# A two-layer graph attention network: the scatter matmuls of a step ahead of the next step's spreading, with index work behind the one-hots

## The chip, the cores and the metric

The kernel runs on one core of one Trainium2 chip. The metric is the time of one execution in microseconds (us); the kernel before takes 4928.91 us (median of three runs, 4916.35 to 4935.57). A core has five engines with an instruction queue each, worked through in order: TensorE (PE in the profile, its weight loads PEld), VectorE (DVE), ScalarE (ACT), GpSimd (POOL) and SyncE (SP). Engines wait for each other by semaphores.

## The reference

A graph attention network of two layers on 6250 nodes with 256 features and 200000 edges, sorted by destination node. Cut to what matters (`src`, `dst` are the edge list, `ea` 32 features per edge; layer 0 has four heads, layer 1 one):

```python
h = maximum(layernorm(x), 0)
for l in (0, 1):
    te  = relu(ea @ We[l] + be[l]) * exp(h @ Wo[l] + bo[l])[src][:, None]
    # one self loop per node, its te the mean of the node's incoming te
    hx  = (h @ Wg[l]).reshape(n, heads, f)
    al  = leaky_relu((hx . a_s)[src] + (hx . a_d)[dst] + (te @ Wge[l]) . a_e, 0.2)
    al  = exp(al - segment_max(al, dst)[dst])
    al /= segment_sum(al, dst)[dst]
    out = segment_sum(hx[src] * al, dst) + b[l]
    h   = relu(out + h) if l == 0 else out + h
return x + (h + maximum(layernorm(x), 0))
```

## The kernel before

**Tiling.** The edges of a layer are cut into chunks of 128 (an edge to a partition), and 24 chunks make a step; 66 steps make a layer (the last two are shorter). Since edges are sorted by destination, the edges of one step belong to a run of at most some hundred nodes, and a node that is cut by a step's border is carried to the next step as one row (`carried`).

**One step** consists of these parts (names of the code; lines of the profile):

- `gather` (L1065): 24 indirect DMAs on POOL fetch the source rows of the edges into `G`, one of three buffers in turn. The gathers of step j+3 use the buffer of step j and wait for its last scatter matmul.
- `spread` (L1189, L1190): one-hots `lb` and `Q` on DVE that spread a node's destination term to its edges, made for two steps at a time; `parts` (L1296 to L1304): that term in three bf16 parts, and a matmul with `Q`; `blocks` (L1311): its result multiplied into `aq`.
- `rphase1` (L1165, L1166): edge features through the edge matrix, `y` on PE and relu into `R` on ACT, in two pieces (256 columns, then 512, called y1 and y2 below). `rphase2` (L1174): `R` through a second matrix into the PSUM bank `zad`. `adst` (L1318): `aq` and `lb` added into the same bank.
- `edge_rows` and `logits` (L1332 to L1363, DVE): `zad` transposed, added to the gathered source terms, leaky relu, and running maxima; `ends` (L1370, PE) transposes chunk ends into the PSUM tile `lf`; `links` (L1380, L1382 DVE, L1387 PE) joins maxima over chunks; `maxima` (L1397 to L1423, DVE, with the exp on ACT) gives each edge its weight.
- `scale` (layer 0: one DVE instruction over all 24 chunks, L1454) or `scale_rows` (layer 1: 24 ACT instructions, L1463) multiplies `G` by the weights; `carried` (L1436 to L1444, DVE) adds the carried row.
- `onehots` (L1283, DVE): `S`, which edge belongs to which node; `sums` (L1473, PE): 24 matmuls of `S` with `G` into `u`, two records each in the profile; `evict` (L1478, ACT) copies `u` out.
- `finish` (DVE, L1489 to L1640 in layer 0, L1494 to L1585 in layer 1): the nodes of a step that is done; in layer 0 `rows1` (L1563 on PE), `rows2` (L567) and `rows3` (L571 on DVE) turn them into the rows that layer 1 gathers. `index_on` (L748 to L779, DVE): up to seven instructions that make the index tables of the next group of four steps, in layer 0 only.

**Order.** The function `edges` writes the instructions of a whole run in program order, and each engine executes its own in that order. The loop is software-pipelined: iteration k finishes step `st` = k (logits onwards) and prepares step `nx` = k+1 (spread, parts, rphase1, rphase2, adst, onehots, edge_rows). In one iteration of the kernel before the order is: gather(nx), logits(st), ends(st), spread(nx), parts(nx), y1(nx), links(st), rows2, blocks(nx), maxima(st), y2(nx), rphase2(nx), adst(nx), scale(st), carried(st), sums(st), rows3, onehots(nx), finish(step k-1), evict(st), rows1(k-1), index_on, edge_rows(nx). The first and the last three steps of a layer have their own sequences.

## Time and profile before

| what | before |
|---|---|
| time, median of three runs | 4928.91 us (4916.35 to 4935.57) |
| the profiled execution | 4925.46 us, span 4923.7 us |
| PE, DVE, POOL, ACT busy | 60%, 50%, 61%, 23% of the span |
| weight loads (PEld), beside the matmuls | 37% |
| mean granted TensorE clock | 0.725 of full speed |
| DMA packets | 248253, 591.97 MB |

No engine is busy all the time, and the busy shares don't say which one sets the pace. In rows of a timeline the first number is the start, the second the busy time of the group, then engine, line, operation, output and inputs, partitions by elements, the count, and in brackets the engine's idle time ahead of the row with what ended it; "issue" there means that the engine waited for nothing that the profile shows.

### The profile page before, as it was taken

Reading aid. Unit: us, or ns where it says so; the run is one execution under the profiler, and the core shown is the slowest. Engines: PE = TensorE matmul, PEld = TensorE weight load, DVE = VectorE, ACT = ScalarE, POOL = GpSimd, SP = SyncE. Lnnn points to the kernel's source line nnn. Section 1 sums busy time; section 2 is a strip of 40 time slices with the busy share of each in tenths; the row PEclk is TensorE's granted clock in tenths of the full one; section 3 lists DMA queues with packets and bytes.
Section 4 is the critical chain, followed back from the end, with each engine's and each line's share of the span. In section 5 each row is a group of like instructions: output and inputs, shape, how many; then the busy total and the mean of one; then the engine's idle time right before and its main releaser. Section 6 shows DMA issues by size and latency. Waiting matters only on the chain.

```text
span 4923.7 us, 38114 instructions
## 1 busy us (share of the span) xinstructions
PE 2940.4 (60%) x10100; PEld 1841.8 (37%) x10100; DVE 2462.7 (50%) x6148; ACT 1132.2 (23%) x2701; POOL 2989.0 (61%) x3216
## 2 busy tenths in 40 slices
PE   6655666666666666665646556555565555655656
PEld 5433433343333434343434333333333333333334
DVE  5556666676666666666734323333333332333335
ACT  4211111111111111111103323233233332323322
POOL 6356666666666666666544656656666666666663
PEclk8777777777777777777777667667667676666767
DMA  7144444444444444444433434434444443443442
GB/s 223 55 119 125 126 128 134 123 135 132 133 124 128 135 126 131 129 135 122 122 109 92 121 106 115 122 105 119 114 118 114 112 121 107 116 118 107 118 117 71
DMA packets 248253, 591.97 MB, mean 120 GB/s; under 512 B 65849, under 2 KB 105125, under 8 KB 247783
## 3 DMA queue, kind: packets, MB, share of 16 engines
q0 software_dynamic: 150048, 422.51, 32.7%
q1 hardware_dynamic: 97009, 164.82, 10.5%
q10 hardware_dynamic: 976, 2.12, 0.2%
q8 instruction: 86, 1.41, 0.1%
q14 instruction: 134, 1.10, 0.1%
HBM read 544.23 MB, written 45.36 MB: 120 GB/s over the span
## 4 chain that ended last, share of the span: by engine, by line
issue 29%; PE 28%; DVE 21%; POOL 13%; another core or an unknown queue 5%; DMA 3%; ACT 1%; SPq 0%; DVEq 0%; ACTq 0%; POOLq 0%
PE u L1473 21%; POOL G L1065 12%; DVE G L1454 7%; DMA G<-T,src 3%; PE y L1165 2%; DVE S L1283 2%; PE zad L1174 2%; DVE m L1402 1%; DVE lb L1189 1%; DVE rt L1332 1%; ACT R L1166 1%; DVE t1rows L1638 1%; DVE fb L1397 0%; PE lf L1370 0%
## 5 line engine op out<-in xcount | busy, mean ns | idle before, releaser
L1065 POOL DMA_INDIRECT G<-T,src x3066 | 2912.9, 950 | 1824.8 <-issue 949.2
L1473 PE MATMUL u<-G,S 128*128 128x270 f32 (+1 forms) x6212 | 1873.3, 448 | 1419.9 <-issue 1202.2
L1473 PEld LDWEIGHTS u<-G,S 128*128 128x128 f32 x6212 | 1355.8, 221 | 1871.8 <-issue 1438.5
L1463 ACT ACTIVATE G<-G,kw 128x256 f32<-128x256 f32 x1512 | 609.0, 496 | 0.0
L1380 DVE TENSOR_TENSOR_SCAN cl<-fl,cl,lf 4x129 f32<-4x129 f32 (+1 forms) x130 | 61.1, 470 | 1007.6 <-PE zad L1304 940.1
L1478 ACT ACTIVATE U<-u 128x270 f32<-128x270 f32 (+1 forms) x130 | 51.0, 393 | 2169.3 <-PE u L1473 1686.5
L1454 DVE TENSOR_TENSOR G<-G,kps 128x6144 f32<-128x6144 f32 (+6 forms) x86 | 441.7, 5150 | 0.0
L1283 DVE TENSOR_TENSOR S<-kps,loc 128x3072 f32<-128x3072 f32 (+1 forms) x135 | 438.1, 3245 | 4.7
L1165 PE MATMUL y<-ea,webd 64*128 64x256 f32 (+2 forms) x1056 | 355.0, 762 | 41.0 <-ACT R L1166 35.3
L1174 PE MATMUL zad<-R,wea 128*64 128x384 f32 (+1 forms) x1056 | 285.0, 677 | 156.6 <-issue 87.5
L1166 ACT ACTIVATE R<-y,webd 128x1024 f32<-128x1024 f32 (+3 forms) x264 | 235.4, 892 | 427.5 <-PE y L1165 161.9
L1174 PEld LDWEIGHTS zad<-R,wea 128*64 128x64 f32 x1056 | 82.9, 177 | 395.8 <-issue 263.4
L1505 DVE SCALAR_TENSOR_TENSOR mg<-U,mw 128x1 f32<-128x1 f32 x65 | 14.4, 221 | 364.1 <-remote 170.6
L1165 PEld LDWEIGHTS y<-ea,webd 64*128 64x128 f32 x1056 | 116.0, 269 | 105.6 <-issue 59.3
L1332 DVE STREAM_TRANSPOSE rt<-zad 128x768 f32<-128x768 f32 (+1 forms) x130 | 125.8, 968 | 5.4 <-remote 5.4
L567 PE MATMUL fin<-wg,h1T 128*128 128x260 f32 x264 | 116.8, 587 | 1.5 <-ACT h1T L1565 1.5
L1189 DVE TENSOR_TENSOR lb<-lb,kps 128x1536 bf16<-128x1536 bf16 (+1 forms) x68 | 112.9, 1661 | 0.0
L1436 DVE SCALAR_TENSOR_TENSOR G<-U,kw,G 1x257 f32<-1x257 f32 x62 | 29.5, 476 | 152.4 <-issue 87.0
L1575 ACT ACTIVATE t1rows<-t1rows 128x1 f32<-128x1 f32 x66 | 13.4, 203 | 363.9 <-DVE t1rows L571 147.4
L1370 PE MATMUL lf<-ident,fb 128*36 128x128 f32 (+1 forms) x132 | 52.0, 394 | 55.8 <-DVE fb L1363 45.6
L1318 PE MATMUL zad<-lb,aq 128*128 128x384 bf16 (+2 forms) x264 | 83.8, 409 | 0.0
L1515 ACT ACTIVATE mw<-mw 128x8 f32<-128x8 f32 x66 | 13.8, 209 | 298.7 <-issue 146.9
(275 smaller groups left out, 2366.7 us busy)
## 6 DMA issues: line engine op xcount, KB each, us to landing
ea<-in_ea_dram SPq DMA_DIRECT2D x64, 768.0 KB
G<-T,src POOLq DMA_INDIRECT x3066
lb<-locrow SPq DMA_DIRECT2D x64, 384.0 KB
nd<-t1rows SPq DMA_DIRECT2D x66, 225.8 KB
tw<-nd SPq DMA_DIRECT2D x66, 225.8 KB
tw<-T SPq DMA_DIRECT2D x66, 117.2 KB
T<-t1rows SPq DMA_DIRECT2D x66, 113.8 KB
tw<-in_x_dram SPq DMA_DIRECT2D x66, 112.0 KB
```

The costliest lines, as they stand in the source:

```text
L567: self.nc.tensor.matmul(ps[:, :L.MW], hT[:, k, :], self.wg[L.l][:, k, :], start=(k == 0), stop=(k == 1))
L1065: nc.gpsimd.indirect_dma_start(out=G[:, c, 0:L.TW], out_offset=None, in_=st.get("from", self.T[L.l])[0:self.N, :], in_offset=bass.Indirect ...
L1165: nc.tensor.matmul(y[:, i, :n], self.webd[l][r, :], ea[r, w], start=True, stop=True)
L1166: nc.scalar.activation(R[:, :, w], y[:, :, :n], AF.Relu, bias=self.be[l])
L1174: nc.tensor.matmul(st["zad"][i * PH:(i + 1) * PH, o], self.wea[l][0], R[:, i, w], start=True, stop=False)
L1189: V.tensor_tensor(lb[:, :, :n], lb[:, :, :n], self.k_part.unsqueeze(2).to_broadcast([P, i, n]), op=OP.is_equal)
L1283: nc.vector.tensor_tensor(st["S"][:, c0:c1, :], self.k_iota.unsqueeze(1).to_broadcast(w), self.loc[:, o + c0:o + c1].unsqueeze(2).to_broad ...
L1318: self.nc.tensor.matmul(st["zad"][:, o], st["aq"].rearrange("p k j -> p (k j)"), st["lb"][:, w], start=False, stop=True)
L1332: V.transpose(rv[:, :32 * c].rearrange("p (b n) -> p b n", b=2), z.rearrange("p (b n) -> p b n", b=2)[:, :, :16 * c])
L1454: nc.vector.tensor_tensor(v, v, pw[:, c0:c1, :].unsqueeze(3) .to_broadcast([P, c1 - c0, H, L.F]), op=OP.mult)
L1463: self.nc.scalar.activation(v, v, AF.Copy, scale=st["w"][:, c:c + 1])
L1473: nc.tensor.matmul(st["u"][:, :L.W], S[:, i, :], G[:, i, 0:L.W], start=(j == 0), stop=(j == c - 1))
```

## The change

In iterations k from 1 on, `links`, `maxima`, the scaling and `carried` of the step come ahead of `spread`, `parts`, `blocks` and `adst` of the next. `parts` then writes its matmul into free columns of the bank of `lf` instead of `zad`. Layer 0 and layer 1 now have different sequences:

- Layer 0: y2 and rphase2(nx) right behind maxima; the scaling in two instructions of 12 chunks with `carried` between them; then spread(nx), 14 chunks of sums, parts(nx), blocks(nx), 5 chunks of sums, adst(nx), the last 5 chunks.
- Layer 1: scale_rows ahead of the second piece of `R`; 8 chunks of sums, with spread and parts of the next step behind them, the other 16 chunks; then rphase2(nx), onehots(nx), blocks(nx) and adst(nx), so that edge_rows(nx) and the next logits, which read `zad`, come behind all of the sums.
- In both, index_on stands right behind the one-hots, ahead of finish, evict and rows1. k = 0 keeps its order.

```diff
--- before.py
+++ after.py
@@ -821,8 +821,9 @@
                 st["rows"] = st["L"].l
                 drain(self.logits(st))
                 self.ends(st)
-            self.spread(nx)
-            self.parts(nx)
+            else:
+                self.spread(nx)
+                self.parts(nx)
             y = self.rphase1(nx)
             next(y)
             if k:
@@ -830,33 +831,59 @@
             if late:
                 self.rows2(late)
             self.load_fl(k + 1)
-            self.blocks(nx)
             if k:
                 drain(self.maxima(st))
-            drain(y)
-            self.load_ea(k + 2)
-            self.rphase2(nx)
-            self.adst(nx)
+            else:
+                self.blocks(nx)
+            if k and st["rows"]:
+                self.scale_rows(st)
+                drain(y)
+                self.load_ea(k + 2)
+            else:
+                drain(y)
+                self.load_ea(k + 2)
+                self.rphase2(nx)
             if "S" not in st:
                 self.onehots(st)
-            if k:
-                if st["rows"]:
-                    self.scale_rows(st)
-                else:
-                    drain(self.scale(st))
+            if not k:
+                self.adst(nx)
+                self.onehots(nx)
+            elif st["rows"]:
                 self.carried(st)
-                self.sums(st)
+                self.sums(st, (0, C // 3))
+                self.spread(nx)
+                self.parts(nx, self.lf)
+                self.sums(st, (C // 3, C))
+                self.rphase2(nx)
+                self.onehots(nx)
+                self.blocks(nx)
+                self.adst(nx)
+            else:
+                f = self.scale(st, cuts=(0, C // 2, C))
+                next(f)
+                self.carried(st)
+                drain(f)
+                self.spread(nx)
+                self.sums(st, (0, 14))
+                self.parts(nx, self.lf)
+                self.blocks(nx)
+                self.sums(st, (14, 19))
+                self.adst(nx)
+                self.sums(st, (19, C))
+                if late:
+                    self.rows3(late)
+                    late = None
+                self.onehots(nx)
             if late:
                 self.rows3(late)
                 late = None
-            self.onehots(nx)
+            self.index_on(left)
             if pv:
                 drain(self.finish(pv))
             self.evict(st)
             if pv:
                 self.rows1(pv)
                 late = pv
-            self.index_on(left)
             if k == 4 and self.early:
                 self.lacking()
             if k >= 6:
@@ -1166,8 +1193,14 @@
             nc.scalar.activation(R[:, :, w], y[:, :, :n], AF.Relu, bias=self.be[l])
             yield
 
+    def zad(self, st):
+
+        if "zad" not in st:
+            st["zad"] = self.ps_1.tile([P, 1024], F32, name="zad")
+
     def rphase2(self, st):
 
+        self.zad(st)
         nc, l, R = self.nc, st["L"].l, st["R"]
         for w, o in self.halves(st):
             for i in range(2):
@@ -1283,7 +1316,7 @@
             nc.vector.tensor_tensor(st["S"][:, c0:c1, :], self.k_iota.unsqueeze(1).to_broadcast(w),
                                     self.loc[:, o + c0:o + c1].unsqueeze(2).to_broadcast(w), op=OP.is_equal)
 
-    def parts(self, st):
+    def parts(self, st, bank=None):
 
         L, V = st["L"], self.nc.vector
         H = L.H
@@ -1300,8 +1333,10 @@
             for j, t in enumerate(q):
                 t["a3"] = a3[:, j]
         a3 = st["a3"]
-        st["zad"] = z = self.ps_1.tile([P, 1024], F32, name="zad")
-        self.nc.tensor.matmul(z[:, 400:400 + 3 * H], st["Q"], a3[:, :H, :].rearrange("p h t -> p (h t)"),
+        if bank is None:
+            self.zad(st)
+        st["ad"] = z = st["zad"][:, 400:400 + 3 * H] if bank is None else bank[:, 240:240 + 3 * H]
+        self.nc.tensor.matmul(z, st["Q"], a3[:, :H, :].rearrange("p h t -> p (h t)"),
                               start=True, stop=True)
 
     def blocks(self, st):
@@ -1309,7 +1344,7 @@
         H = st["L"].H
         st["aq"] = aq = self.aq[st["k"] % 2]
         self.nc.vector.tensor_tensor(aq[:, :, 4:4 + 3 * H],
-                                     st["zad"][:, 400:400 + 3 * H].unsqueeze(1).to_broadcast([P, 4, 3 * H]),
+                                     st["ad"].unsqueeze(1).to_broadcast([P, 4, 3 * H]),
                                      self.quad.unsqueeze(2).to_broadcast([P, 4, 3 * H]), op=OP.mult)
 
     def adst(self, st):
```

In layer 0, PE's queue reads so before, from a step's end to its sums (u is the scatter's sum, y and R the edge features, zad the edge terms, fin the node rows):

```order
L1563 MATMUL fin<-ident,fb 128x128 x2
L1370 MATMUL lf<-ident,fb_195 36x128
L1304 LDWEIGHTS Q
L1304 MATMUL zad<-a_6577,Q 128x12
L1165 MATMUL y<-ea,webd_119 128x256 x2
L1387 MATMUL lf<-ident,cl_189 128x36
L567 MATMUL fin<-wg_894,h1T 128x260 x2
L1165 MATMUL y<-ea,webd_119 128x512 x2
L1174 MATMUL zad<-R,wea_142 64x384 x4
L1318 LDWEIGHTS aq_199
L1318 MATMUL zad<-lb,aq_199 128x384
```

and so after, from y2 on (L1192 is the old L1165, L1207 the old L1174, L1508 the sums, L1339 parts, L1353 adst):

```order
L1192 MATMUL y<-ea,webd_119 128x512 x2
L1207 MATMUL zad<-R,wea_142 64x384 x4
L1508 MATMUL u<-G,S 128x270 x14
L1339 LDWEIGHTS Q
L1339 MATMUL lf<-a_7320,Q 128x12
L1508 MATMUL u<-G,S 128x270 x5
L1353 LDWEIGHTS aq_198
L1353 MATMUL zad<-lb,aq_198 128x384
L1353 LDWEIGHTS aq_198
L1353 MATMUL zad<-lb,aq_198 128x384
L1508 MATMUL u<-G,S 128x270 x5
```

The parts matmul and the adst matmuls have moved from ahead of the sums into them; DVE's `blocks`, which needs the former, therefore waits for 14 chunks of sums.

DVE's queue in layer 0, in a step without spreading, from the scaling on, before:

```order
L1454 TENSOR_TENSOR G<-G,kps 128x24x256
L1439 TENSOR_TENSOR crow<-U,kps 1x256
L1442 TENSOR_TENSOR crow<-U,kps 1x4
L1443 TENSOR_TENSOR G<-G,crow 1x260
L1444 SCALAR_TENSOR_TENSOR G<-U,slink,G 1x5
L571 TENSOR_TENSOR t1rows<-fin,bias_898 128x260
L1280 COPY kps<-lastloc 128x1
L1283 TENSOR_TENSOR S<-kps,loc 128x3072
L1489 TENSOR_SCALAR cnt<-U 128x1
```

and after (L1489 is now the scaling, L1346 blocks, L1316 the one-hots, L748 the first instruction of index work):

```order
L1489 TENSOR_TENSOR G<-G,kps 128x12x256
L1474 TENSOR_TENSOR crow<-U,kps 1x256
L1477 TENSOR_TENSOR crow<-U,kps 1x4
L1478 TENSOR_TENSOR G<-G,crow 1x260
L1479 SCALAR_TENSOR_TENSOR G<-U,slink,G 1x5
L1489 TENSOR_TENSOR G<-G,kps 128x12x256
L1346 TENSOR_TENSOR aq_199<-lf,quad 128x4x12
L571 TENSOR_TENSOR t1rows<-fin,bias_898 128x260
L1313 COPY kps<-lastloc 128x1
L1316 TENSOR_TENSOR S<-kps,loc 128x3072
L748 CAST gf<-gi 128x192
```

The row of `blocks` now stands ahead of everything that DVE does for node rows, one-hots and the next logits; before, it stood ahead of maxima.

PE's queue in layer 1, one step, before:

```order
L1370 MATMUL lf<-ident,fb_195 33x128
L1304 LDWEIGHTS Q
L1304 MATMUL zad<-a_12796,Q 128x3
L1165 MATMUL y<-ea,webd_900 128x256 x2
L1387 MATMUL lf<-ident,cl_189 128x33
L1165 MATMUL y<-ea,webd_900 128x512 x2
L1174 MATMUL zad<-R,wea_145 64x384 x4
L1318 LDWEIGHTS aq_199
L1318 MATMUL zad<-lb,aq_199 128x384
L1318 LDWEIGHTS aq_199
L1318 MATMUL zad<-lb,aq_199 128x384
L1473 MATMUL u<-G,S 128x261 x24
```

and after:

```order
L1508 MATMUL u<-G,S 128x261 x8
L1339 LDWEIGHTS Q
L1339 MATMUL lf<-a_21417,Q 128x3
L1508 MATMUL u<-G,S 128x261 x16
L1207 MATMUL zad<-R,wea_145 64x384 x4
L1353 LDWEIGHTS aq_199
L1353 MATMUL zad<-lb,aq_199 128x384
L1353 LDWEIGHTS aq_199
L1353 MATMUL zad<-lb,aq_199 128x384
L1405 MATMUL lf<-ident,fb_195 33x128
L1192 MATMUL y<-ea,webd_900 128x256 x2
```

The matmuls into zad of the next step (its own rows aside, the same number) stand behind the sums, directly ahead of the transpose L1405 (before: L1370) that needs the logits made from them.

## The prediction

> **What bounds the kernel now.** First the page, its chain and its costliest groups.
>
> ```profile
> issue 29%; PE 28%; DVE 21%; POOL 13%; another core or an unknown queue 5%; DMA 3%; ACT 1%; SPq 0%; DVEq 0%; ACTq 0%; POOLq 0%
> L1473 PE MATMUL u<-G,S 128*128 128x270 f32 (+1 forms) x6212 | 1873.3, 448 | 1419.9 <-issue 1202.2
> ```
>
> No engine owns the chain. The sums carry most of PE's idle time, and it is put down to "issue": PE waits for nothing that the profile shows. So I looked at the beat of the steps, in the timeline of POOL: the first gather of a step, first and last regular step of layer 0, then of layer 1.
>
> ```profile
> 335.12 0.94 POOL L1065 DMA_INDIRECT G<-T,src  x1 [24.97 <-PE fin L1563]
> ...
> 1229.18 0.94 POOL L1065 DMA_INDIRECT G<-T,src  x1 [4.61 <-PE fin L1563]
> ...
> 1258.39 0.95 POOL L1065 DMA_INDIRECT G<-T,src  x1 [0.30 <-issue]
> 1267.51 0.94 POOL L1065 DMA_INDIRECT G<-T,src  x1 [8.18 <-PE u L1473]
> ...
> 1301.98 0.94 POOL L1065 DMA_INDIRECT G<-T,src  x1 [4.62 <-PE fin L1563]
> ...
> 2374.07 0.99 POOL L1065 DMA_INDIRECT G<-T,src  x1 [5.59 <-PE u L1473]
> ...
> 2699.18 0.94 POOL L1065 DMA_INDIRECT G<-T,src  x1 [8.29 <-PE zad L1304]
> ...
> 4801.97 0.94 POOL L1065 DMA_INDIRECT G<-T,src  x1 [7.21 <-PE zad L1304]
> ```
>
> Layer 0: 2038.95 us in 57 steps, 35.77 each. Layer 1: 2102.79 us in 58 steps, 36.25 each. A step's 24 gathers run back to back at 1.25 us, about 30 us (1229.2 to 1259.3 here); then POOL waits until the sums of the step that holds its next buffer end. I call the time from burst start to burst start T, and the time from burst start to the first sums matmul S. A faster S only pays if it ends the sums earlier, so next the sums in PE's timeline, layer 0, a late step and an ordinary one:
>
> ```profile
> 1244.87 9.93 PE L1473 MATMUL u<-G,S 128*128 128x270 f32 x36 [3.30 <-DVE G L1444]
> ...
> 1263.03 4.21 PE L1473 MATMUL u<-G,S 128*128 128x270 f32 x9 [1.49 <-issue]
> ...
> 1279.01 11.99 PE L1473 MATMUL u<-G,S 128*128 128x270 f32 x45 [4.59 <-DVE crow L1442]
> ...
> 1297.20 0.61 PE L1473 MATMUL u<-G,S 128*128 128x270 f32 x1 [2.41 <-issue]
> ...
> 1301.59 0.42 PE L1370 MATMUL lf<-ident,fb 128*36 128x128 f32 x1
> ```
>
> This is the central observation. 45 of 48 records run in 12 us; then they come 2.8 us apart, until some 3.5 us after the last gather, and after that what is left runs fast again (9 records in 4.2 us). I call it the slow stretch; the trace shows it on all queues, not its cause. Two bounds on a step follow. The late step (S = 1244.87-1229.2 = 15.7) still has 9 records when the stretch ends, and T is 38.3. The ordinary one (S = 11.5) is done at 1297.8, half a microsecond after the burst, and gains nothing by it: PE gets on at 1301.6 and POOL at 1302.0, T = 34.5. In the steps of layer 0 T never falls under 34.4; I take 34.45 as a floor. Of 57 steps 15 have T over 37 (mean 38.39), the other 42 a mean of 34.84.
>
> For the cause of a late S, DVE's timeline:
>
> ```profile
> 1230.55 0.33 DVE L1363 TENSOR_TENSOR_SCAN fb<-pen,al 128x96 f32<-128x96 bf16 x1
> ...
> 1233.48 0.47 DVE L1380 TENSOR_TENSOR_SCAN cl<-fl,cl,lf 4x129 f32<-4x129 f32 x1
> ...
> 1267.92 0.47 DVE L1380 TENSOR_TENSOR_SCAN cl<-fl,cl,lf 4x129 f32<-4x129 f32 x1 [1.41 <-PE zad L1304]
> ...
> 1271.43 6.54 DVE L1454 TENSOR_TENSOR G<-G,kps 128x6144 f32<-128x6144 f32 x1
> ...
> 1278.74 0.20 DVE L1444 SCALAR_TENSOR_TENSOR G<-U,slink,G 1x5 f32<-1x5 f32 x1
> ...
> 1289.93 0.98 DVE L1332 STREAM_TRANSPOSE rt<-zad 128x768 f32<-128x768 f32 x1
> ...
> 1299.61 0.33 DVE L1363 TENSOR_TENSOR_SCAN fb<-pen,al 128x96 f32<-128x96 bf16 x1
> ```
>
> In the late step DVE ends the logits at 1230.9, 1.7 after the burst began, and spreads for 2.7 ahead of links. In the ordinary one it was done in time, and the chain is links, maxima, scaling, carried: 1267.9 to 1278.9. DVE has little to spare: from 1289.93 the last eight instructions of the logits take 10 us, in the slow stretch.
>
> **The change in layer 0.** Half of the scaling goes behind carried: 6.54/2 = 3.27 off the path. blocks (short, 0.2 as L1444) and, in every second step, spread and the parts casts (2.7) leave the path to links. So S falls from 11.5 to about 8.0, if the logits are in time. Two costs stand against it.
>
> DVE's cover: blocks now waits for the parts matmul behind 28 records, 28 x 12/45 = 7.5 us from S, so at +15.8 in a step; the one-hots and the node rows, which began at 1278.9 (+11.4), begin at about +16, 4.6 later, and the second half of the scaling and the spreading (6.0) lie in that gap. Everything behind them, logits last, moves to the right, into the slow stretch. Before, the logits ended at +32.4 (1299.9); now I expect some +35, and with seven instructions of index work +37 or +38 (before, such a step had them 1.7 past the next burst's start: the late step above). Against T = 34.5 they are 0.5 to 3.5 late, which gives S = 8.5 to 11.5, not 8.0.
>
> PE: parts (two instructions) and adst lie in the sums; the number of instructions ahead of the last sums matmul is the same, so I count nothing, bounds 0 and +1 a step.
>
> S of 8.5 to 11.5 is where T stood at 34.4 to 35. I take 34.75 for all 57: 57 x (35.77-34.75) = -58. Bounds: all at the floor, 57 x 1.32 = -75; or DVE so late that S is 12 to 13 everywhere, where T was about 36 in the few steps of before that started so: 57 x 0.23 = +13.
>
> index_on goes ahead of finish (7 x 0.3, with L1363 for a short instruction, is 2 us) and no longer stands between finish and edge_rows: the same queue, the same sum, 0 for the logits, but rows1 on PE comes 2 later; PE waits for the logits there anyway. rows3 keeps its place behind the sums, and so do its stores on SP. Of load_ea and load_fl on SP only the place in layer 1 changes, behind the scaling; they fetch a later step's data, 0. One scaling more costs one instruction's start, covered by DVE's wait for blocks. No row of POOL's queue moves.
>
> **The change in layer 1.** Here zad and adst leave the front of the sums and come behind them. Burst starts of a step with fast and one with slow matmuls ahead of its sums, then PE in the latter, all engines in the former, and its logits:
>
> ```profile
> 3644.12 0.94 POOL L1065 DMA_INDIRECT G<-T,src  x1 [7.25 <-PE zad L1304]
> ...
> 3679.13 0.94 POOL L1065 DMA_INDIRECT G<-T,src  x1 [5.21 <-PE zad L1304]
> ...
> 4112.78 0.94 POOL L1065 DMA_INDIRECT G<-T,src  x1 [7.28 <-PE zad L1304]
> ...
> 4149.45 0.94 POOL L1065 DMA_INDIRECT G<-T,src  x1 [6.90 <-PE zad L1304]
> ```
>
> ```profile
> 4118.01 2.83 PE L1174 MATMUL zad<-R,wea 128*64 128x384 f32 x8 [1.22 <-issue]
> ...
> 4120.78 0.82 PE L1318 MATMUL zad<-lb,aq 128*128 128x384 bf16 x2
> ...
> 4121.39 8.56 PE L1473 MATMUL u<-G,S 128*128 128x261 f32 x37
> ...
> 4145.94 3.25 PE L1473 MATMUL u<-G,S 128*128 128x261 f32 x6 [2.23 <-issue]
> ...
> 4149.30 0.70 PE L1165 MATMUL y<-ea,webd 64*128 64x256 f32 x4
> ```
>
> ```profile
> 3644.09 0.47 DVE L1380 TENSOR_TENSOR_SCAN cl<-fl,cl,lf 1x129 f32<-1x129 f32 x1 [12.33 <-PE zad L1304]
> ...
> 3646.26 0.23 ACT L1419 ACTIVATE kw<-mt 128x25 f32<-128x25 f32 x1 [0.77 <-DVE mt L1410]
> ...
> 3647.73 9.66 ACT L1463 ACTIVATE G<-G,kw 128x256 f32<-128x256 f32 x24
> 3647.89 1.51 PE L1174 MATMUL zad<-R,wea 128*64 128x384 f32 x8 [1.22 <-ACT R L1166]
> ...
> 3648.66 0.20 DVE L1444 SCALAR_TENSOR_TENSOR G<-U,slink,G 1x2 f32<-1x2 f32 x1
> ...
> 3649.33 0.50 PE L1318 MATMUL zad<-lb,aq 128*128 128x384 bf16 x2
> 3649.66 8.53 PE L1473 MATMUL u<-G,S 128*128 128x261 f32 x38
> ```
>
> ```profile
> 3659.26 0.97 DVE L1332 STREAM_TRANSPOSE rt<-zad 128x768 f32<-128x768 f32 x1
> ...
> 3661.69 0.18 DVE L1363 TENSOR_TENSOR_SCAN fb<-pen,al 128x24 f32<-128x24 bf16 x1
> ```
>
> Before, S is 5.5 (3649.66-3644.12) with T = 35.0, or 8.6 (4121.39-4112.78) with T = 36.7; of the 58 steps 11 are of the first kind, 36 of the second, and 11 lie between at S = 7.3 with T about 35.6. The mean S is 7.8.
>
> New chain from the last sums matmul: zad and adst 1.51+0.5 = 2.0 to 2.83+0.82 = 3.65, with two handovers 2.3 to 3.9; edge_rows and logits 3659.26 to 3661.87 = 2.6; the transpose 0.4 (as 1301.59) and links up to kw's end 3644.09 to 3646.49 = 2.4; the first row's scaling 0.5 (ACT L1463, 9.66 us for 24, is now ahead of R) and carried 0.7. Sum 8.9 to 10.5; I take 9.7, a delay of 1.9. Before, DVE had made the logits during the sums and then stood idle for 12.33; that cover is gone, and nothing else hides them.
>
> What does a later S cost here? From S = 5.5 to 8.6 T rose by 1.7, about 0.5 per microsecond; counted by records less: 37 run fast, the slow stretch ends at the same time after the burst, so 1.9 us later means 0.7 of a 2.8-us record less done in it and 0.3 to 0.5 more behind. I take 0.65 per step: 58 x 0.65 = +38. Bounds: 0.25 (+15) and 1.45 (+84, if every step gets S = 10.5 and 0.5 per microsecond).
>
> A rule bears on the lower bound. The Trainium skill, "TensorE: Matmul & The Clock Gate" (Part 1: The HAM clock gate), says that the array runs at half rate until it was busy for about 3.4 us. The trace agrees: behind 3.25 us of sums (4145.94) the next y took 0.70, while the zad of 4118.01, behind a wait, took 2.83 against 1.51. By that rule zad, run right behind the tail of the sums, would warm up by itself, and the term would be that for S = 8.9, some +25 rather than +38.
>
> **The sum.** -58 + 38 = -20 for the profiled execution: 4925.46 - 20 = 4905; that execution lies 3.4 under the median, so 4909 on the median's scale. What lies outside the regular steps (prologue, turn, endings) keeps its order: 0.
>
> A difference under 0.5% (24.6 us) I call the same.
>
> **The rivals.**
>
> (a) Slower: DVE's wait for the parts matmul takes the place of the spreading. If its node rows and logits (28 instructions, 35 with index work) meet the slow stretch at one in 1.25 us (eight in 10), the logits end 4 to 5 after the burst start in every step, and S is 12 to 13: layer 0 +13, layer 1 +38 to +50: 4929 + 55 = about 4984. It decides from logits at +38 on. For it: before, a step has only the 1.41 us ahead of 1267.92 to spare. Against it: behind the stretch DVE's remaining instructions take 0.3 each.
>
> (b) Faster: in layer 1 T hangs on the end of the slow stretch, not on S (0.25 a step), and layer 0 comes near its floor: 4929 - 70 + 12 = 4871. For it: fewer than ten records stand behind the stretch in any step.
>
> (c) The sums start early enough, or zad's twelve records out of their way let more of them run ahead of the stretch, so that all end before it: all steps at 34.45, 57 x 1.32 + 58 x 1.8 = -180: 4749. The Trainium skill, "Runtime: NRT & Kernel Launch" (Instruction fetch mechanics), has instruction fetching mostly hidden behind issue; by it nothing would hold 48 records back once they have their data. The rows with 2.4 us "issue" between single matmuls speak against it. In layer 1 the count of PE instructions per step is unchanged, so no more of them come ahead.
>
> (d) Nothing moves: steps are pinned by burst and stretch in both layers, 4929. Against it: the 15 steps with T over 37, all late starts.
>
> **How the numbers follow.** My forecast 0.42 (its own range 4870 to 4945: 0.18 faster, 0.17 same, 0.07 slower); (a) 0.26, of it 0.24 slower; (b) 0.21, faster; (c) 0.04, faster; (d) 0.07, same. Faster 0.43, same 0.26, slower 0.31. The range 4855 to 4985 takes in (b) and the middle of (a), and leaves out (c) and the worst of (a).
>
> **What the profile after would show.** Right: layer 0 bursts 34.75 us apart with the beat of 38 every fourth step gone, sums starting 8.5 to 11.5 after them; layer 1 bursts 36.9 apart, the sums starting 9 to 10.6 after; DVE idle about 2 to 5 us per layer 0 step ahead of blocks, ended by the parts matmul. Wrong: sums in layer 0 still 12 or more behind the burst with DVE busy (rival a); layer 1's T unchanged although its S grew (b). It would also be wrong if the slow stretch began earlier, counted from another point than the burst.

## The result: slower by 5%, and the profile after

| | before | after |
|---|---|---|
| time, median of four runs | 4927.24 us | 5181.84 us |
| ratio | | 1.0519 (95% interval 1.0487 to 1.0551) |
| profiled execution, its span | 4925.46 us, 4923.7 us | 5194.46 us, 5192.7 us |
| layer 0, per step (57 steps) | 35.77 us | 39.97 us |
| layer 1, per step (58 steps) | 36.25 us | 36.43 us |

The change makes the kernel 5.2% slower; the forecast was 4909 us, with a range up to 4985. The layers are read from POOL's timeline of the changed kernel, as before: the first gather of the first and of the last step of layer 0, then of layer 1; between them one step's burst and the start of the next.

```profile
337.38 0.94 POOL L1092 DMA_INDIRECT G<-T,src  x1 [21.94 <-PE u L1508]
...
1257.27 1.01 POOL L1092 DMA_INDIRECT G<-T,src  x1 [11.14 <-PE u L1508]
...
1296.85 0.94 POOL L1092 DMA_INDIRECT G<-T,src  x1 [9.60 <-PE u L1508]
...
2615.74 0.94 POOL L1092 DMA_INDIRECT G<-T,src  x1 [9.11 <-PE u L1508]
...
2954.51 0.94 POOL L1092 DMA_INDIRECT G<-T,src  x1 [8.09 <-PE u L1508]
...
5067.65 0.95 POOL L1092 DMA_INDIRECT G<-T,src  x1 [7.47 <-PE u L1508]
```

Layer 0: (2615.74-337.38)/57 = 39.97. Layer 1: (5067.65-2954.51)/58 = 36.43. Of the 269 us between the two profiled executions layer 0 holds 239, layer 1's regular steps 10, the turn between the layers 14 (338.8 against 325.1), and start and end 6.

The page of the changed kernel names the place, in its costliest groups:

```profile
L1346 DVE TENSOR_TENSOR aq<-lf,quad 128x12 bf16<-128x12 f32 (+1 forms) x125 | 24.0, 192 | 2023.9 <-remote 1720.5
```

This is blocks: 24 us of work in both layers, and DVE idle for 2024 us ahead of it, 16 us each time. "remote" in such a row means that the end of no instruction in the profile matches the moment at which the wait ended. One step in layer 0, in DVE's timeline and in PE's, with the last gather of its burst in POOL's:

```profile
1276.87 0.18 DVE L1332 TENSOR_TENSOR a<-a3r,a 128x8 bf16<-128x8 f32 x1
1291.70 0.21 DVE L1346 TENSOR_TENSOR aq<-lf,quad 128x48 bf16<-128x48 f32 x1 [14.66 <-remote]
...
1292.35 3.36 DVE L1316 TENSOR_TENSOR S<-kps,loc 128x3072 f32<-128x3072 f32 x1
...
1303.46 0.33 DVE L1398 TENSOR_TENSOR_SCAN fb<-pen,al 128x96 f32<-128x96 bf16 x1
```

```profile
1271.16 6.65 PE L1508 MATMUL u<-G,S 128*128 128x270 f32 x28
1277.65 0.17 PE L1339 MATMUL lf<-a,Q 128*128 128x12 bf16 x1
1277.68 1.39 PE L1508 MATMUL u<-G,S 128*128 128x270 f32 x5
...
1291.97 0.82 PE L1353 MATMUL zad<-lb,aq 128*128 128x384 bf16 x2 [2.19 <-DVE aq L1346]
```

```profile
1286.31 0.95 POOL L1092 DMA_INDIRECT G<-T,src  x1 [0.30 <-issue]
```

The matmul that blocks waits for was over at 1277.8, and DVE was free at 1277.0. DVE starts at 1291.7. Nothing else is waited for: the instruction has one semaphore to wait for, PE's. The trace's list of updates of that semaphore shows where the 14 us went. PE sends one behind the last matmul of `zad` (over at 1271.24), one for each of the 14 chunks and one for the parts matmul, 16 that are due between 1271.2 and 1277.8. The list has 15, at (us):

```
1274.36 1282.16 1287.05 1289.86 1291.26 1291.31 1291.35 1291.39
1291.43 1291.47 1291.52 1291.56 1291.60 1291.64 1291.68
```

Four in 17 us, then eleven within 0.42, and blocks 0.02 behind the last. Matmuls that take 0.39 us each can't have ended 0.04 us apart: they were done, and their signals were held up. The list isn't whole, though. In this run it has 2551 of PE's 2980 updates and 3558 of DVE's 5133; on a chip without the slow stretch, below, it lacks eight at most of either. So which update is missing can't be told, and when blocks starts is the surer evidence. In all layer 0 steps blocks starts 34.1 to 34.6 behind the burst's start, 4.0 to 4.8 behind the end of its last gather, whether the parts matmul ran at +20 or at +32. Everything DVE has behind it, one-hots, node rows and logits, comes after that. In the step above the logits were to be ready at 1296.85, the next burst's start; DVE had then just begun the node rows, and the logits (L1398) ended at 1303.8.

Layer 1 has the same hold-up, and it costs little there. PE's and DVE's timeline of one step, which began at 3718.75:

```profile
3733.70 0.17 PE L1339 MATMUL lf<-a,Q 128*128 128x3 bf16 x1
```

```profile
3752.66 0.18 DVE L1346 TENSOR_TENSOR aq<-lf,quad 128x12 bf16<-128x12 f32 x1 [21.85 <-PE u L1508]
```

The signal takes 18.8 us, to +33.9, but there only adst, behind the sums anyway, waits for blocks.

### The profile page after: what moved, and what is told of

The parts are those of the page before. It is cut to its first block, busy times and chain, and to the rows that moved or that the text cites. A ratio compares the mean times of both kernels' runs of the same rounds, so it can differ in the third digit from the quotient of the medians.

```text
span 5192.7 us, 38155 instructions
## 1 busy us (share of the span) xinstructions
PE 3095.6 (60%) x10100; PEld 1879.2 (36%) x10100; DVE 2472.3 (48%) x6210; ACT 1136.2 (22%) x2701; POOL 2995.2 (58%) x3216
## 4 chain that ended last, share of the span: by engine, by line
DVE 24%; PE 22%; another core or an unknown queue 21%; issue 19%; POOL 9%; DMA 3%; ACT 2%; DVEq 0%; ACTq 0%; SPq 0%; POOLq 0%
PE u L1508 14%; POOL G L1092 9%; DVE G L1489 6%; DVE S L1316 3%; PE y L1192 3%; DMA G<-T,src 2%; DVE rt L1367 1%; DVE lb L1222 1%; PE ps L567 1%; PE zad L1207 1%; DVE m L1437 1%; PE lf L1405 1%; PE fin L567 1%; DVE al L1385 0%
## 5 line engine op out<-in xcount | busy, mean ns | idle before, releaser
L1508 PE MATMUL u<-G,S 128*128 128x270 f32 (+1 forms) x6212 | 1944.7, 459 | 1039.1 <-issue 892.3
L1508 PEld LDWEIGHTS u<-G,S 128*128 128x128 f32 x6212 | 1372.4, 226 | 1652.9 <-issue 1184.1
L1346 DVE TENSOR_TENSOR aq<-lf,quad 128x12 bf16<-128x12 f32 (+1 forms) x125 | 24.0, 192 | 2023.9 <-remote 1720.5
L1489 DVE TENSOR_TENSOR G<-G,kps 128x3072 f32<-128x3072 f32 (+7 forms) x148 | 450.1, 3049 | 0.0
L1316 DVE TENSOR_TENSOR S<-kps,loc 128x3072 f32<-128x3072 f32 (+1 forms) x135 | 438.0, 3245 | 4.7
L1192 PE MATMUL y<-ea,webd 64*128 64x256 f32 (+2 forms) x1056 | 397.9, 848 | 38.9 <-issue 22.7
L1207 PE MATMUL zad<-R,wea 128*64 128x384 f32 (+1 forms) x1056 | 288.7, 685 | 113.9 <-issue 66.8
L1405 PE MATMUL lf<-ident,fb 128*36 128x128 f32 (+1 forms) x132 | 50.2, 380 | 425.0 <-DVE fb L1398 249.2
L1538 ACT ACTIVATE mw<-mw,mg 128x2 f32<-128x2 f32 x66 | 19.6, 298 | 972.6 <-DVE mg L1537 944.2
L1207 PEld LDWEIGHTS zad<-R,wea 128*64 128x64 f32 x1056 | 86.9, 184 | 328.2 <-issue 222.6
L1405 PEld LDWEIGHTS lf<-ident,fb 128*36 128x36 f32 (+1 forms) x132 | 15.0, 114 | 478.2 <-DVE fb L1398 282.2
L1598 PE MATMUL fin<-ident,fb 128*128 128x128 f32 x132 | 39.5, 395 | 247.1 <-ACT fb L1587 202.6
L1192 PEld LDWEIGHTS y<-ea,webd 64*128 64x128 f32 x1056 | 124.1, 287 | 116.7 <-issue 93.3
L567 PE MATMUL fin<-wg,h1T 128*128 128x260 f32 x264 | 134.7, 664 | 1.5 <-ACT h1T L1600 1.5
L1598 PEld LDWEIGHTS fin<-ident,fb 128*128 128x128 f32 x132 | 17.1, 180 | 276.4 <-ACT fb L1587 226.5
L1353 PE MATMUL zad<-lb,aq 128*128 128x384 bf16 (+2 forms) x264 | 89.0, 431 | 38.0 <-DVE aq L1346 37.8
```

The source lines that it names most:

```text
L567: self.nc.tensor.matmul(ps[:, :L.MW], hT[:, k, :], self.wg[L.l][:, k, :], start=(k == 0), stop=(k == 1))
L1192: nc.tensor.matmul(y[:, i, :n], self.webd[l][r, :], ea[r, w], start=True, stop=True)
L1207: nc.tensor.matmul(st["zad"][i * PH:(i + 1) * PH, o], self.wea[l][0], R[:, i, w], start=True, stop=False)
L1316: nc.vector.tensor_tensor(st["S"][:, c0:c1, :], self.k_iota.unsqueeze(1).to_broadcast(w), self.loc[:, o + c0:o + c1].unsqueeze(2).to_broad ...
L1405: self.nc.tensor.transpose(self.lf[0:e.shape[1], 1:P + 1], e, self.ident)
L1489: nc.vector.tensor_tensor(v, v, pw[:, c0:c1, :].unsqueeze(3) .to_broadcast([P, c1 - c0, H, L.F]), op=OP.mult)
```

## The experiments

The experiments ran on five different chips; that of the result above is not on record. They fall into two kinds, which must be told apart to read any number here. On three of the five, as on that of the result, the kernel before takes 4860 to 4927 us and has the slow stretch. On the other two it takes 4016 to 4022 us, and there is no stretch and no gap: in the kernels run there with gathers at full pace, gathers run on from step to step, 30.0 to 30.3 us a step. Each kernel is compared with the kernel before on the same chip. Steps in microseconds are means over the regular steps of a layer, from the first gathers, as above.

| kernel | stretch | before there | time | ratio (95%) | layer 0 | layer 1 |
|---|---|---|---|---|---|---|
| e_layer1 | no | 4015.87 | 4018.95 | 1.0004 (0.9995 to 1.0014) | | |
| e_layer0 | no | 4015.87 | 4022.40, one run | 1.0016 | | |
| e_parts_first | no | 4015.87 | 4015.71 | 1.0002 (0.9993 to 1.0012) | | |
| e_no_wait | no | 4015.87 | 4014.86, one run | 0.9997 | | |
| r_after | yes | 4860.20 | 5129.36 | 1.0547 (1.0508 to 1.0585) | 39.5 | 35.8 |
| r_parts_first | yes | 4860.20 | 4913.48 | 1.0103 (1.0068 to 1.0137) | 36.2 | 35.7 |
| r_no_wait | yes | 4860.20 | 4958.32, one run | 1.020 | 36.5 | 36.0 |
| e_pause | yes | 4860.20 | 5169.81, one run | 1.064 | 38.1 | 38.1 |
| w_halves | yes | 4869.87 | 4870.95 | 0.9998 (0.9989 to 1.0008) | 35.4 | 35.7 |
| w_signals_first | yes | 4869.87 | 4877.67 | 1.0015 (1.0004 to 1.0027) | 35.5 | 35.7 |
| e_paced_before | yes | 4869.87 | 4884.73 | 1.0030 (1.0017 to 1.0043) | 35.4 | 35.8 |
| e_paced_after | yes | 4869.87 | 5151.46 | 1.0574 (1.0553 to 1.0595) | 39.9 | 35.9 |
| e_slow_gathers | no | 4017.23 | 5534.73, one run | 1.378 | 42.0 | 42.5 |
| e_blocks_late | no | 4017.23 | 4013.33 | 0.9991 (0.9980 to 1.0002) | | |
| r_blocks_late | yes | 4917.44 | 5060.00 | 1.0283 (1.0239 to 1.0326) | 38.0 | 36.2 |
| r_slow_gathers | yes | 4917.44 | 5661.94, one run | 1.151 | 42.5 | 42.5 |
| w_paced2 | no | 4021.62 | 4560.74 | 1.1339 (1.1320 to 1.1357) | 34.4 | 34.4 |
| e_paced2_after | no | 4021.62 | 4557.59 | 1.1330 (1.1308 to 1.1353) | 34.4 | 34.4 |

### One layer at a time

Each takes the new order in one layer and the old one in the other (e_layer1 shown; e_layer0 has `not st["rows"]`):

```diff
-            else:
+            new = k and st["rows"]
+            if not new:
                 self.spread(nx)
                 self.parts(nx)
...
-            if k and st["rows"]:
+            if new and st["rows"]:
                 self.scale_rows(st)
```

> Layer 1 in the new order, layer 0 as before (index work stays behind the one-hots). Theory W: the loss comes from layer 0 alone, where DVE's blocks stands at a wait for the parts matmul in the middle of the sums. Then layer 0 is back at 35.8 us a step and layer 1 keeps its 36.4: 4927 + 58 x 0.2 = about 4940. Rival B: both layers' new orders cost, layer 1's hidden behind the same mean: about 4980 or more.

> The complement: layer 0 in the new order, layer 1 as before. Theory W: about 5170, layer 0 at 40 us a step, layer 1 at 36.25. Rival B: clearly under 5130.

Both met a chip without the stretch, and neither order costs anything there that can be told (the 0.16% of e_layer0 is one run), so they don't divide the loss; the trace of the changed kernel did that. What they do show is that there is no loss where there is no stretch. The timeline of e_layer0, PE and DVE, with layer 0 in the new order:

```profile
1037.53 6.65 PE L1519 MATMUL u<-G,S 128*128 128x270 f32 x28
1044.02 0.17 PE L1350 MATMUL lf<-a,Q 128*128 128x12 bf16 x1
```

```profile
1044.25 0.21 DVE L1357 TENSOR_TENSOR aq<-lf,quad 128x48 bf16<-128x48 f32 x1 [0.74 <-PE lf L1350]
```

blocks (L1357) follows 0.06 us behind the parts matmul (L1350). The updates of PE's semaphore come as the matmuls end: zad's at 1037.51, the chunks' 14 from 1038.26 to 1044.19, 0.46 apart, and the parts matmul's at 1044.22.

### The parts matmul first, and no wait at all

```diff
                 self.carried(st)
-                drain(f)
                 self.spread(nx)
-                self.sums(st, (0, 14))
                 self.parts(nx, self.lf)
                 self.blocks(nx)
-                self.sums(st, (14, 19))
+                drain(f)
+                self.sums(st, (0, 19))
                 self.adst(nx)
```

> Both layers in the new order, but in layer 0 spread, parts and blocks come behind carried and ahead of the second half of the scaling and of all sums, so that blocks waits for a matmul that is not behind sums. Theory W: DVE stands nowhere, layer 0 at about 34.8 us a step: 4927 - 57 x 1 + 11 = about 4880. Rival D: it is not this wait but the rest of the order (adst inside the sums, DVE's work moved to behind the scaling) that meets the slow stretch: layer 0 stays over 38 us a step, over 5050.

> As before for this kernel. With the slow stretch, theory W: 0.98 to 1.0 of before, layer 0 at 34.6 to 35.5 us a step. Rival D: over 1.03. Without the stretch: 1.00.

The kernel without the wait has a constant tile in the place of the parts matmul's output, and so leaves out layer 0's destination terms:

```diff
                 self.parts(nx, self.lf)
+                nx["ad"] = self.ident[:, 0:12]
                 self.blocks(nx)
```

> The changed kernel, except that blocks in layer 0 reads a constant tile in place of the parts matmul's output (the destination terms of layer 0 are left out so), which takes away what it waits for; every instruction stays in its place. Theory W: blocks runs straight behind the scaling or the spreading, layer 0 at 34.7 to 35.5, in all 4880 to 4930. Rival D: unchanged, 5180.

> As before for this kernel (blocks of layer 0 reads a constant tile, the destination terms of layer 0 are left out). With the slow stretch, theory W: 0.98 to 1.0 of before; rival D: 1.05. Without the stretch: 1.00.

> The changed kernel once more, to see on which kind of chip these runs stand: on the first chip the kernel before took 4927 us with steps of 35.8 us and gathers followed by 4 to 9 us of POOL idleness; on the second 4016 us with steps of 30.0 to 30.3 us and no such gap. If the slow stretch late in each burst is there: 1.052 of before. If not: within 0.3% of before, since all waits then lie under the gathers.

With the stretch the changed kernel is again 5.5% slower. The parts matmul put first takes 216 of its 269 us away: layer 0 from 39.5 to 36.2 us a step. It is not the gain that theory W had, and the kernel without any wait for blocks stays at 36.5. So something is left, in both. DVE's and PE's timeline of the former:

```profile
1046.16 0.49 PE L1352 MATMUL zad<-lb,aq 128*128 128x384 bf16 x2
```

```profile
1058.15 0.98 DVE L1366 STREAM_TRANSPOSE rt<-zad 128x768 f32<-128x768 f32 x1 [11.14 <-remote]
```

It is the same thing once more. adst (L1352) still stands in the sums, its last matmul is over at 1046.6, and edge_rows (L1366) gets to know at 1058.15, 34.1 behind the burst's start at 1024.0 and 4.05 behind the end of its last gather at 1054.10. The logits then end 2.9 us behind the next burst's start in about every second step.

### All signals ahead of the sums, and the halves alone

w_signals_first starts from the kernel with the parts matmul first and puts adst ahead of the sums too (layer 1 in the old order):

```diff
                 self.parts(nx, self.lf)
                 self.blocks(nx)
+                self.adst(nx)
                 drain(f)
-                self.sums(st, (0, 19))
-                self.adst(nx)
-                self.sums(st, (19, C))
+                self.sums(st)
```

> Layer 1 as before; layer 0 as in the kernel with parts and blocks ahead of the sums, and adst ahead of them too, so that no engine waits for a matmul in or behind the sums. With the slow stretch, theory S (a matmul's signal given late in a burst is held up until some 4 us behind its last gather): the transpose into edge_rows no longer starts at +34 but in the middle of the burst, layer 0 under 35.5 us a step: 0.985 to 1.0 of before. Rival, that the rest of the new order costs: over 1.005. Without the stretch: 1.00.

w_halves takes only the scaling in two halves into the kernel before:

```diff
-                    drain(self.scale(st))
-                self.carried(st)
+                    f = self.scale(st, cuts=(0, C // 2, C))
+                    next(f)
+                    self.carried(st)
+                    drain(f)
                 self.sums(st)
```

> The kernel before with one part of the change alone: in layer 0 the scaling in two halves with carried between them. All matmuls that another engine waits for stay ahead of the sums. Where the slow stretch is there: S falls by 3.3 us in every layer 0 step, the fifteen late steps fall from 38.4 to some 36.5, the others stay at their floor of 34.5: 0.990 to 0.996 of before. Rival: the ends of the sums hang on the stretch alone, 1.00. Without the stretch: 1.00.

With no engine waiting for a matmul in the sums, layer 0 is back at 35.5 us and the kernel at 1.0015 of before: the two late signals are the whole loss of layer 0, to some 0.15% of the kernel's time. But there is no gain either. The halves did what they should: the sums start 9.7 us behind the burst's start in the mean over layer 0, where they start 12.8 behind it in e_paced_before, which has the old order on the same chip. T is 35.4 in both. The rival of that line was right: three microseconds of S buy nothing. PE's timeline and POOL's of w_halves, two steps:

```profile
1206.69 10.38 PE L1476 MATMUL u<-G,S 128*128 128x270 f32 x41
1218.78 0.39 PE L1476 MATMUL u<-G,S 128*128 128x270 f32 x1 [1.72 <-issue]
...
1230.70 1.25 PE L1476 MATMUL u<-G,S 128*128 128x270 f32 x2 [0.81 <-issue]
```

```profile
1196.93 0.94 POOL L1068 DMA_INDIRECT G<-T,src  x1 [4.73 <-PE zad L1307]
...
1232.22 0.94 POOL L1068 DMA_INDIRECT G<-T,src  x1 [5.38 <-PE u L1476]
```

S = 9.8, 41 records run fast, and the last ones come at 1230.7 all the same, 4 us behind the burst, when the stretch ends. An earlier start only meets the stretch earlier.

Even sums that end ahead of the stretch gain nothing. In another step of w_halves all 48 records run fast (PE, then POOL, then ACT, which copies u out):

```profile
424.22 11.21 PE L1476 MATMUL u<-G,S 128*128 128x270 f32 x48 [1.36 <-DVE crow L1445]
```

```profile
416.20 0.94 POOL L1068 DMA_INDIRECT G<-T,src  x1 [8.39 <-PE u L1476]
...
450.53 0.97 POOL L1068 DMA_INDIRECT G<-T,src  x1 [4.21 <-remote]
```

```profile
450.29 0.40 ACT L1481 ACTIVATE U<-u 128x270 f32<-128x270 f32 x1 [14.55 <-remote]
```

The sums are over at 435.43. ACT and POOL, which wait for PE's semaphore alone, start at 450.29 and 450.53: 15 us later, and again some 4 behind the last gather. Nine of the 57 steps are like this, with 11 to 15 us of delay. So the floor of some 34.4 us a step is the same hold-up, of the signal that lets POOL begin its next burst.

### Where the hold-up comes from

e_pause puts 40 small memsets between gather 20 and 21:

```diff
+            if n == 20 and st["k"] > 8:
+                for _ in range(40):
+                    nc.gpsimd.memset(self.scr, 0.0)
+            n += 1
             nc.gpsimd.indirect_dma_start(
```

> The changed kernel with 40 small memsets on POOL between gather 20 and 21 of a step, in a scratch tile, some 4 to 10 us in which no gather is issued. With the slow stretch: theory S, that signals between engines are held up while gathers are issued, has blocks start inside the pause, 25 to 33 us behind the burst's start; rival, that the hold-up ends a fixed time behind the last gather, has it start behind gather 24 plus 4.4 us as in the changed kernel. Without the stretch: each step longer by the memsets, 126 times 4 to 10 us, if POOL sets the pace.

POOL's, PE's and DVE's timeline:

```profile
1051.24 0.94 POOL L1098 DMA_INDIRECT G<-T,src  x1 [0.30 <-issue]
...
1059.99 0.95 POOL L1098 DMA_INDIRECT G<-T,src  x1
```

```profile
1046.77 0.17 PE L1345 MATMUL lf<-a,Q 128*128 128x12 bf16 x1
```

```profile
1056.10 0.21 DVE L1352 TENSOR_TENSOR aq<-lf,quad 128x48 bf16<-128x48 f32 x1 [12.61 <-remote]
```

POOL no longer waits at the border of a step; the pause of 7.8 us between 1052.2 and 1060.0 is now the only one, in the middle of a step's gathers, and 24 gathers lie between two pauses. blocks (L1352) starts in the pause, 3.9 us after the last gather ahead of it, as it did behind the burst in the changed kernel. So the hold-up ends because gathers stop, not because the step ends. By step time (38.1 in both layers: 30 of gathers and 8 of pause) this kernel is even ahead of the changed one in layer 0; in layer 1 it loses.

Then the pace. One memset ahead of each gather, in both kernels:

```diff
+            if st["k"] > 8:
+                nc.gpsimd.memset(self.scr, 0.0)
             nc.gpsimd.indirect_dma_start(
```

> The kernel before with one small memset on POOL, 0.17 us, ahead of every gather from the tenth step on, so that gathers come every 1.42 us in place of 1.25. With the slow stretch, theory P, that the hold-up is a backlog that gathers at full pace pile up: the stretch is gone or shorter, steps of 34.1 us (24 x 1.42) in both layers in place of some 35.5: 0.955 to 0.97 of before. Rival: the hold-up is there whatever the pace, and every step is longer by up to 4 us: 1.03 to 1.10. Without the stretch: 126 x 24 x 0.17 = 514 us longer, 1.12.

> The changed kernel, paced in the same way. With the slow stretch, theory P: as fast as the paced kernel before, within 1%, since blocks then gets its signal when the matmul ends. Rival: 1.05 or more of the paced kernel before.

That test failed as a test: the memset fits into the 0.30 us between two gathers, which stay 1.26 apart (1200.14, 1201.40, 1202.66 in POOL's timeline). Both kernels are where they were, 1.003 and 1.057. Four memsets:

```diff
-                nc.gpsimd.memset(self.scr, 0.0)
+                for _ in range(4):
+                    nc.gpsimd.memset(self.scr, 0.0)
```

> The changed kernel with four small memsets on POOL ahead of every gather from the tenth step on (one was swallowed by the 0.30 us between gathers): gathers some 1.75 us apart, a burst of 42 us. Theory P, a backlog that gathers at 1.25 us pile up: blocks follows the parts matmul within 2 us and POOL goes from one burst into the next without the gap of 4 us, steps of 42 us in both layers. Rival, a hold-up at any pace: blocks starts some 4 us behind the last gather, at +46, and the steps are 46 us and more.

> As before for this kernel; without the stretch it took 5535 us, paced by gathers 1.7 us apart. With the stretch: theory P, a backlog that gathers at 1.25 us pile up: about the same time, blocks within 2 us of the parts matmul wherever DVE is free. Rival, a hold-up at any pace: blocks some 4 us behind the last gather, and 123 times 4 us more, about 6000.

With the stretch, POOL's, PE's and DVE's timeline of the changed kernel, so slowed:

```profile
1241.51 0.95 POOL L1096 DMA_INDIRECT G<-T,src  x1
1242.46 0.63 POOL L1095 MEMSET scr<- 128x16 f32 x4
1243.24 0.95 POOL L1096 DMA_INDIRECT G<-T,src  x1
```

```profile
1239.62 4.03 PE L1512 MATMUL u<-G,S 128*128 128x270 f32 x17
1243.49 0.17 PE L1343 MATMUL lf<-a,Q 128*128 128x12 bf16 x1
1243.52 2.52 PE L1512 MATMUL u<-G,S 128*128 128x270 f32 x10
```

```profile
1243.70 0.21 DVE L1350 TENSOR_TENSOR aq<-lf,quad 128x48 bf16<-128x48 f32 x1 [3.49 <-PE lf L1343]
```

Gathers 1.73 apart, and the hold-up is gone on a chip that has it at 1.25: blocks follows the parts matmul by 0.06 us in the median over the run, PE runs on without gaps, and at a step's border POOL loses half a microsecond. The run has its own comparison, too. The memsets begin only with the tenth step, and ahead of them gathers come at 1.25. POOL's, PE's and DVE's timeline of the last such step:

```profile
417.22 0.95 POOL L1096 DMA_INDIRECT G<-T,src  x1 [11.43 <-PE u L1512]
...
456.76 0.95 POOL L1096 DMA_INDIRECT G<-T,src  x1 [8.97 <-PE u L1512]
```

```profile
439.08 0.17 PE L1343 MATMUL lf<-a,Q 128*128 128x12 bf16 x1
```

```profile
451.55 0.21 DVE L1350 TENSOR_TENSOR aq<-lf,quad 128x48 bf16<-128x48 f32 x1 [15.75 <-remote]
```

Here blocks is 12.3 us late, and the step takes 39.5, as in the changed kernel. From 456.76, the first paced burst, to the first gather of the last regular step of layer 1 this run takes 5088.4 us, and the same kernel on a chip without the stretch takes 5087.2: once gathers are slow, the two kinds of chips run alike, and nearly all of the 127 us between the two runs lies ahead of that. So the hold-up goes with the pace of the gathers. A kernel with two memsets, meant for a pace of 1.43 (1.40 was measured), was to show whether that is enough and whether it beats both kernels:

> The kernel before with two small memsets on POOL ahead of every gather from the tenth step on: gathers some 1.43 us apart. With the slow stretch, where 24 gathers and the gap behind them never took less than 34.4 us, which is 1.43 us for each: theory P, a service that takes 1.43 us a gather and a backlog at any faster pace: the backlog never forms, steps of 34.4 us in both layers without late signals, 0.965 to 0.975 of before. Rival: the gap comes on top of the longer burst, 1.04 to 1.08. On a chip without the stretch: 4.2 us more a step, 1.12 to 1.13.

> The changed kernel, paced in the same way. With the stretch, theory P: blocks follows the parts matmul at once, within 1.5% of the paced kernel before. Rival: 1.05 or more of before, blocks behind the burst as in the changed kernel. Without the stretch: 1.12 to 1.13.

It met a chip without the stretch and cost there what the longer bursts cost, 13%, in the old order and the new alike. What it does with the stretch stays open.

### Signal, or instructions?

```diff
                 self.sums(st, (0, 14))
                 self.parts(nx, self.lf)
-                self.blocks(nx)
-                self.sums(st, (14, 19))
-                self.adst(nx)
-                self.sums(st, (19, C))
+                self.sums(st, (14, C))
...
             if pv:
                 drain(self.finish(pv))
+            if k and not st["rows"]:
+                self.blocks(nx)
+                self.adst(nx)
             self.evict(st)
```

> The changed kernel, but in layer 0 blocks stands on DVE behind the one-hots, the index work and the node rows, and adst on PE behind all sums; the parts matmul stays in the middle of the sums. Theory S, that only the matmul's signal is held up: DVE goes on with the one-hots and node rows while it is, and only blocks, adst and the logits (some 5 us) come behind the burst: layer 0 at 37 to 38 us a step, 1.02 to 1.03 of before. Rival, that DVE itself gets no instructions in that time: the node rows come behind the burst as well, layer 0 at 39.5 to 40, 1.05.

> As before for this kernel, which met a chip without the slow stretch (0.999 of before there). With the stretch: theory S, only the matmul's signal is held up, layer 0 at 37 to 38 us a step, 1.02 to 1.03 of before; rival, DVE gets no instructions, 39.5 to 40, 1.05.

With the stretch 1.028 and 38.0 us a step, the upper end of what theory S had. DVE's timeline, and one row each of PE and ACT:

```profile
1042.28 3.36 DVE L1316 TENSOR_TENSOR S<-kps,loc 128x3072 f32<-128x3072 f32 x1
...
1047.28 0.16 DVE L1552 TENSOR_TENSOR mg<-U,mw 128x4 f32<-128x4 f32 x1 [0.28 <-issue]
...
1051.31 0.43 DVE L1675 TENSOR_TENSOR t1rows<-t1rows,fb 128x256 f32<-128x256 f32 x1 [1.32 <-DVE t1rows L1673]
1060.57 0.21 DVE L1346 TENSOR_TENSOR aq<-lf,quad 128x48 bf16<-128x48 f32 x1 [8.83 <-remote]
```

```profile
1045.12 0.17 PE L1339 MATMUL lf<-a,Q 128*128 128x12 bf16 x1
```

```profile
1047.03 0.21 ACT L1550 ACTIVATE mw<-mw 128x8 f32<-128x8 f32 x1 [4.62 <-DVE mw L1549]
```

In a burst that began at 1026.6, DVE goes through the one-hots and all node rows while the signal of the parts matmul (over at 1045.3) is held, and only blocks waits for it, until 1060.57. So DVE has its instructions; it lacks PE's signal. Not all signals are held up alike: meanwhile ACT answers DVE, and DVE goes on 0.04 us behind ACT's end (1047.24 to 1047.28). DVE's own signals, on which its dependent instructions wait, come within 0.04 us up to 1049.6 and 1.32 late at 1051.31; in w_halves one was 4.36 late. And PE itself is slowed in a way that no signal explains: in the stretch it idles up to 3.1 us between two matmuls of the sums, also where they wait for nothing.

## Why the prediction was wrong, step by step

**The floor and the gaps were read rightly; what they mean was not.** Bursts of 30 us, the stretch until some 3.5 to 4.8 us behind the last gather, and a T that never falls under some 34 (34.4 in the trace of before, 34.05 in r_parts_first) hold in every run with the stretch and with gathers at full pace. The prediction left the cause open and treated the stretch as instructions that come slowly, each engine for itself. PE's records do come slowly there, and why stays open; what cost the time is a delay of PE's signals, gone where gathers come more slowly, and it strikes every engine that waits for PE.

**The failed step is "DVE's cover" in layer 0.** It has blocks at "+15.8 in a step" and the one-hots "at about +16", that is, the signal taken as given when the matmul ends. The matmul was on time by that account (+20.4 in the step shown, S being 13.9); the signal came at +34.4. Logits expected at +35 to +38, 0.5 to 3.5 us late for a T of 34.5, ended at +46.2 to +48.9, over 11 late by that measure; S became 16.7 in the mean in place of 8.5 to 11.5, and the term of -58 us measured +239. Rival (a) had the right place, DVE's wait for the parts matmul, and the right sign, but took its price from DVE's speed in the stretch; at +13 for layer 0 it was short by 226, and the range ended at 4985.

Could it have been seen? The trace of before shows no wait of DVE, late in a burst, for a matmul inside the sums; so the price of such a wait was not in it, and the bounds were drawn from DVE's instructions that wait for their own engine. But the clue stood in rows that the prediction shows. In its ordinary step the last sums matmul is over at 1297.8 (1297.20 and 0.61), POOL's next burst waits for that matmul, and it starts at 1301.98, 4.2 us later (its row names fin, the matmul that ended last ahead of it). The prediction took this for a floor and did not ask what POOL waited for. In 26 of the 57 steps POOL starts over 2 us behind the end of the sums, in 28 it is 0.27. A wait of a kind that the trace does not hold should have had the whole burst as its upper bound: blocks at +34.4, 18.6 us later than assumed.

**That a smaller S shortens the step failed too,** hidden under the larger loss. w_halves has the gain in S and none in T. In the trace of before, late starts and long steps went together, but the start was not the cause: in r_parts_first steps with an S of 11.2 to 11.4 take 34.3 us or 38.4. That both came of DVE being late would fit, but no run varies that alone.

**Layer 1: right in direction, too dear.** +38 predicted, +10 measured, 0.18 a step. S rose to 9.7 as worked out, in the mean of the steps (the chain from zad over the logits was priced rightly; its zad took 2.4 us in the mean, 1.6 to 2.9). The step that failed is the slope of T in S, 0.65 a step for 1.9 us; rival (b), in which T hangs on the stretch, had 0.25 and fits better. No run varies S in layer 1 alone.

**The sum's other terms** (index work, rows3, load_ea, the extra scaling) were put at 0; w_signals_first, which has all of them in layer 0, is within 0.15% of before, so that holds for them together. Rival (c) spoke of fetching: the Trainium skill, "Runtime: NRT & Kernel Launch" (Instruction fetch mechanics), holds it to be hidden mostly. For DVE the runs agree, since in r_blocks_late it worked on in the stretch, one-hots and node rows from 1042.28 to 1051.7, while PE's signal was held; for PE, whose records come 2.8 us apart there without a wait, no run shows it.

**Rival (d),** no change at all, is what happens on the chips without the stretch, as far as the parts of the change were run there: 1.0004 and 1.0016. There POOL issues gathers without a pause (30.0 to 30.3 us a step), and all that the change moves lies under them.

## What to carry to other kernels

Before a waiting instruction is moved, ask how long its signal takes at the new place, not only when its producer ends: a wait that the old profile never held at that place has no price in it, and its upper bound is the end of whatever congests that stretch. Where a long run of matmuls meets such a stretch, put what another engine needs ahead of it, and keep behind the wait on an in-order queue only what really needs it; blocks late cost 2.8% where blocks in front of everything cost 5.2 to 5.5%. And look at how the end of a step moves with its start in an experiment, before a correlation in the trace is taken as a slope.

## What the runs showed of the hardware

- On some chips PE's signals came 10 to 20 us late to DVE, ACT and POOL while GpSimd issued indirect gathers back to back: of sixteen updates of PE's semaphore, due within 6.6 us, the trace has four in 17 us and eleven in 0.42. At 1.73 us a gather they were on time, in the same run in which they had been 12 us late at 1.25. The hold-up ended some 4 us behind the last gather, in the middle of a step's gathers, too, if there was a pause.
- Chips differ. Of the five on record three had it and two had not, with the same kernel at 4860 to 4917 us and at 4016 to 4022; only one was used twice, and it was without both times. Whether it belongs to the chip or to something else of the session was not varied. A change can cost 5% on one and nothing on another.
- With the stretch 24 gathers and the gap behind them take at least 34.05 to 34.4 us, which would be 1.42 to 1.43 us a gather against an issue at 1.25; that some service runs at this rate and backs up would fit it, but was not shown. What is backed up is open, too; DMA landings and instruction fetching were not varied.
- The profiler is a rival that stays. All executions here were recorded by it, and with the stretch its own records are thinned out: the trace of the changed kernel lists 13648 landings of DMAs, the same gathers without the stretch some 60500 (e_no_wait 60488). If the recording of signals is what backs up, a run that isn't recorded may have neither the stretch nor the loss; no such run was made.
- Four memsets of 128x16 take 0.63 us on POOL, and one costs next to nothing between two gathers, which leave 0.30 us: they come 1.26 apart in place of 1.25.
